# Elementwise sums of y and of W that the planner may give to GpSimd as well as to VectorE

## Chip, core and metric

The kernel runs on one core of a Trainium2 chip. The metric is the device time of one execution in microseconds (us); the median of three runs is quoted. Within the core, TensorE (PE in the profile) multiplies, VectorE (DVE), ScalarE (ACT) and GpSimd (POOL) do elementwise work, and SyncE (SP) issues the DMAs.

## What is computed

The reference, cut to what matters, for two batches of 1024 tokens with 2048 features:

```python
q1 = fake_quant(_layernorm(x), x1_scale, x1_zp)
q2 = fake_quant(ctx_4096, x2_scale, x2_zp)
x = x + jnp.matmul(q1, q2)                      # first product, 2048 x 2048 per batch

n = _layernorm(x)
logits = n @ W_router.T                         # 8 experts, softmax, best 2, weights w
h = jnp.einsum('td,erd->ter', n, lora_A)        # rank 16 per expert
lora = jnp.einsum('ter,eor,te->to', h, lora_B, w) * SCALING
x = x + n @ W_base.T + b_base + lora            # second product, 2048 x 2048
```

## The kernel before

The inputs are fp32; TensorE gets fp16. In the second product each operand is split into a high and a low fp16 part and three products (high x low, low x high, high x high) are accumulated, so each block costs three matmuls. To save matmuls the second product (and the first one of the second batch) uses a Strassen-like scheme: tokens, features and output columns are halved, and seven products of sums and differences take the place of eight. Those sums are what this change is about:

- **Sums of y.** After the second layer norm `y_prep` makes, for each pair p of token tiles, four fp32 tiles of 128 x 1024 (a11, a12, a21, a22) and from them s1, s2, s3 and s4, with four sums by `comb` (L917). `emit` then makes the high part (`affine`, on ACT or DVE), the low part (L910 on DVE), and a DMA transpose.
- **Sums of W.** `w_step(S, b, cp, grp, k)` makes one step's weights: for each of two batches b, two column halves cp, four groups grp and eight k. It loads tiles of W, forms none, one or two sums (L1085 to L1141; 512 or 1024 columns), then the high part `hi` (`affine`, L386 on ACT or L393 on DVE) and the low part `lo` (L1070, a scalar_tensor_tensor on DVE with two SBUF operands).

`g2` then multiplies (L1258) with four token pairs per step; the last k of a group adds the LoRA matmuls (L1274) and evicts PSUM with L1286 on DVE. The accumulators X and Y of four pairs use all eight PSUM banks, so a fresh group waits for the evictions of the one before.

All work is given to a planner, `Plan`, as tasks with estimated durations. A task may be for one engine or for several (`durs` is a dictionary of engine and duration). `rank` gives each task its latest start `prio`, counted back from the matmuls' planned times over durations and hops of 0.7 us (`HOP`). `order` then simulates the engines: at each event it goes over SP, ACT, DVE, POOL and PE in this order, and each free engine takes the ready task with the earliest `prio` that fits into the tile slots. `lag` is how far PE runs behind its planned times. The resulting order is static: each engine executes its own list in order, and semaphores hold it where data is late. Before the change, the only tasks with two engines are for ACT and DVE, and DVE leaves them to ACT when that is free:

```python
if eng == "DVE" and len(t.durs) > 1 and busy["ACT"] <= now:
    continue
```

POOL has only set-up work and the Newton steps of the inverse square root (L432 to L443, then L644 to L646 or L887 to L889), instructions on one or two columns. The work of a batch runs in this order: first product (gemm1), second layer norm and y preparation, router and the first column half of W (cp = 0), second column half (cp = 1), while the next batch is loaded and normalised.

Of the kernel before, what the change touches and what calls it, by code (L numbers as in the profile page):

```python
# [17 lines left out]
ALU = mybir.AluOpType  # L18
# [14 lines left out]
C = 512  # L33
# [49 lines left out]
TURN_LAND = 0.65  # L83
TURN_COST = 0.75
NEXT = {"DVE": 0.08, "ACT": 0.1}


class Buf:
# [18 lines left out]
class Plan:  # L107
# [56 lines left out]
    def order(self):  # L164
# [52 lines left out]
        while todo:  # L217
            if not events:
                raise RuntimeError("no progress")
            nxt = heapq.heappop(events)  # L220
            if nxt <= now:
                continue
            now = nxt
            while releases and releases[0][0] <= now:
                free[heapq.heappop(releases)[-1].tag] += 1
            for eng in busy:
                while busy[eng] <= now:
                    pick = None
                    q = ready[eng]
                    for n, item in enumerate(q):  # L230
                        t = item[2]
                        if t.ready > now:
                            continue
                        h = t.far if t.far is not None else HORIZON
                        if t.prio + lag > now + h:
                            wake(t.prio + lag - h)
                            if t.prio + lag > now + HORIZON:
                                break
                            continue
                        if t.dma is not None:  # L240
                            if dma_free > now + DEPTH:
                                wake(dma_free - DEPTH)
                                break
                            if len([x for x in lanes if x > now]) >= LANES:
                                break
                        if eng == "DVE" and len(t.durs) > 1 and busy["ACT"] <= now:
                            continue
                        if not fits(t):
                            continue
                        pick = t  # L250
                        break
                    if pick is None:
                        break
                    t = pick
                    t.eng, t.dur = eng, t.durs[eng]
                    for e in t.durs:
                        ready[e].remove((t.prio, t.seq, t))
                    for tag, n in t.need.items():
                        free[tag] -= n
                        queue[tag].remove(t)  # L260
                    held.update(t.bufs)
                    t.start = now
                    end = now + t.dur
                    if t.dma is not None:
                        if t.turn:
                            end = max(end, land - 0.2)
                        dma_free = max(end + 0.2, dma_free) + t.dma
                        t.done = dma_free + (
                            TURN_LAND if t.turn else STORE_LAND if t.store else LAND
                        )  # L270
                        land = max(land, t.done)
                        lanes = [x for x in lanes if x > now] + [t.done]
                    else:
                        t.done = end + 0.1
                        end -= NEXT.get(eng, 0.0)
                    busy[eng] = end
                    wake(end)
                    wake(t.done)
                    if t.pe is not None:
                        lag = now - t.pe  # L280
                    for b in t.bufs:
                        b.users -= 1
                        if b.tag in free:
                            b.last = max(getattr(b, "last", 0.0), t.done)
                            if not b.users:
                                heapq.heappush(releases, (b.last, next(count), b))
                                wake(b.last)
                    for s in t.succs:
                        s.left -= 1
                        s.ready = max(s.ready, t.done)  # L290
                        if not s.left:
                            for e in s.durs:
                                bisect.insort(ready[e], (s.prio, s.seq, s))
                            wake(s.ready)
                    todo -= 1
# [4 lines left out]
def xattn_ffn_kernel(ctx, tc, x, cx, scal, wT, bias, arT, bT, out):  # L300
# [78 lines left out]
    def affine(dst, src, n, r, w, scale=None, bias=None, only=None, **kw):  # L379
# [20 lines left out]
        if only:  # L400
            return add(only, durs[only], lambda: fn(only), r=r, w=w, **kw)
        return add(durs, 0, fn, r=r, w=w, **kw)

    def stats(b, s, j, h):
        st = s.ap()[:, j * 24 : (j + 1) * 24].rearrange("p (c s) -> p c s", c=NC)
# [487 lines left out]
    def y_prep(S, b, p):  # L893
# [20 lines left out]
                lambda: n.ap().rearrange("p h c -> p (h c)"), [n], [y], D)  # L914

        def comb(dst, a, c, op):
            add("DVE", 1.22, lambda: nc.vector.tensor_tensor(dst.ap(), a.ap(), c.ap(), op),  # L917
                r=[a, c], w=[dst])

        t1 = norm("a11", 0, 0)  # L920
        emit("a11", t1)
# [135 lines left out]
    def w_step(S, b, cp, grp, k):  # L1057
# [17 lines left out]
        if not cp:  # L1075
            if grp == 0:
                s = kept.pop((cp, k), None) or load_wcol(k, cp, 0, f"wc_{n}", far=WFAR)
            elif grp == 1:
                top = load_wrow(k, cp, f"wt_{n}", far=WFAR)
                s = buf("u", [P, HD], F32, f"wb_{n}", 2)  # L1080
                load(s, lambda: s.ap()[:, :C],
                     wT[(HK + k) * P : (HK + k + 1) * P, cp * HD + C : (cp + 1) * HD],
                     C * 4, [(s, [0])])
                add("DVE", 0.69,
                    lambda: nc.vector.tensor_tensor(  # L1085
                        s.ap()[:, C:], top.ap()[:, C:], top.ap()[:, :C], ALU.subtract),
                    r=[top], w=[(s, [1])])
                add("DVE", 0.69,
                    lambda: nc.vector.tensor_tensor(
                        s.ap()[:, :C], s.ap()[:, :C], s.ap()[:, C:], ALU.subtract), w=[s])  # L1090
            elif grp == 2:
                s = load_wcol(k, cp, 1, f"wc_{n}", far=WFAR)
                add("DVE", 0.69,
                    lambda: nc.vector.tensor_tensor(  # L1094
                        s.ap()[:, :C], s.ap()[:, C:], s.ap()[:, :C], ALU.subtract), w=[s])
            else:
                top = load_wrow(k, cp, f"wt_{n}", far=WFAR)
                s = load_wrow(HK + k, cp, f"wb_{n}", far=WFAR)
                add("DVE", 1.22,
                    lambda: nc.vector.tensor_tensor(s.ap(), s.ap(), top.ap(), ALU.subtract),  # L1100
                    r=[top], w=[s])
                add("DVE", 0.69,
                    lambda: nc.vector.tensor_tensor(
                        s.ap()[:, :C], s.ap()[:, :C], s.ap()[:, C:], ALU.subtract), w=[s])
            hi(lambda: s.ap()[:, :m], 0, m, [s])
            lo(lambda: s.ap()[:, :m], 0, m, [s])
            return
# [5 lines left out]
            return  # L1113
        top = load_wrow(k, cp, f"wt_{n}", far=WFAR)
        if grp == 0:
            add("DVE", 0.69,
                lambda: nc.vector.tensor_tensor(
                    top.ap()[:, C:], top.ap()[:, C:], top.ap()[:, :C], ALU.subtract), w=[top])
            hi(top.ap, 0, HD, [top])
            lo(top.ap, 0, HD, [top])  # L1120
        elif grp == 1:
            bot = buf("u", [P, HD], F32, f"wb_{n}", 2)
            load(bot, lambda: bot.ap()[:, C:],
                 wT[(HK + k) * P : (HK + k + 1) * P, cp * HD + C : (cp + 1) * HD],
                 C * 4, [(bot, [1])])
            add("DVE", 0.69,
                lambda: nc.vector.tensor_tensor(
                    bot.ap()[:, :C], top.ap()[:, :C], top.ap()[:, C:], ALU.subtract),
                r=[top], w=[(bot, [0])])
            add("DVE", 0.69,  # L1130
                lambda: nc.vector.tensor_tensor(  # L1131
                    bot.ap()[:, :C], bot.ap()[:, :C], bot.ap()[:, C:], ALU.add), w=[bot])
            hi(bot.ap, 0, HD, [bot])
            lo(bot.ap, 0, HD, [bot])
        else:
            bot = load_wrow(HK + k, cp, f"wb_{n}", far=WFAR)
            add("DVE", 1.22,
                lambda: nc.vector.tensor_tensor(bot.ap(), bot.ap(), top.ap(), ALU.subtract),
                r=[top], w=[bot])
            add("DVE", 0.69,  # L1140
                lambda: nc.vector.tensor_tensor(  # L1141
                    bot.ap()[:, :C], bot.ap()[:, :C], bot.ap()[:, C:], ALU.subtract), w=[bot])
            hi(bot.ap, 0, HD, [bot])
            lo(bot.ap, 0, HD, [bot])

# [297 lines left out]
```

## Time and profile before

| what | value |
|---|---|
| median of 3 runs | 927.47 us (926.11 to 927.49) |
| profiled execution | 930.89 us, span of its instructions 929.1 us |
| DVE busy | 763.4 us, 82% of the span |
| ACT busy | 418.1 us, 45% |
| POOL busy | 88.8 us, 10% |
| mean granted TensorE clock | 0.992 |

The page gives busy time by engine, and groups of instructions by line, engine and shape with their count, total and mean duration and the idle time of their engine just before them. PEld is the weight load of TensorE. A wait is written "engine line <- what ended it". Idle time of an engine that is not the bottleneck costs nothing by itself.

### The profile page before, as it was taken

The page shows a single profiled execution, that of the slowest core. Times are in us where ns is not written, and L with a number is a line of the kernel's source. Part 1 is how long each engine was busy: PE and PEld are TensorE (multiplying, and loading weights), DVE is VectorE, ACT ScalarE, POOL GpSimd, SP SyncE. Part 2 cuts the span into 40 slices and gives each one's busy share as a digit, 9 for nine tenths or more (in the row PEclk, how much of TensorE's full clock was granted, in tenths as well). Part 3 has the DMA queues.
Part 4 walks back from the last instruction along what each step waited for, and adds up shares of the span by engine and source line. Part 5 has one row for each costly group of instructions (what it writes and reads, how often), then busy time and mean ns, then how long its engine had stood idle before and what let it go on. Part 6 is the DMA issues. An engine that isn't in the chain of part 4 may idle for free.

```text
span 929.1 us, 12550 instructions
## 1 busy us (share of the span) xinstructions
PE 901.3 (97%) x4514; PEld 431.5 (46%) x4514; DVE 763.4 (82%) x1300; ACT 418.1 (45%) x475; POOL 88.8 (10%) x337
## 2 busy tenths in 40 slices
PE   7899998999989999999999999999999999999998
PEld 5444445474434444444444444547443444444443
DVE  7899969999588886999689988899889895699231
ACT  5899558615155331334594665851523221234000
POOL 1425230000000000004440004000000000000000
PEclk8999999999999999999999999999999999999999
DMA  8999999898999998957899926999997879893021
GB/s 321 388 383 265 301 283 249 144 226 279 228 320 320 389 366 289 400 198 246 256 329 277 347 105 178 246 239 221 303 219 244 260 236 382 294 371 119 18 89 48
DMA packets 223183, 241.03 MB, mean 259 GB/s; under 512 B 152464, under 2 KB 154512, under 8 KB 223120
## 3 DMA queue, kind: packets, MB, share of 16 engines
q1 hardware_dynamic: 223120, 240.23, 84.9%
q8 instruction: 35, 0.57, 0.2%
q14 instruction: 28, 0.23, 0.1%
HBM read 172.03 MB, written 31.46 MB: 219 GB/s over the span
## 4 chain that ended last, share of the span: by engine, by line
PE 74%; DVE 10%; DMA 10%; issue 2%; POOL 2%; ACT 1%; SPq 1%; DVEq 0%; POOLq 0%; ACTq 0%
PE X L1258 30%; PE Y L1258 22%; PE g L725 8%; PE gX L845 5%; PE gY L845 3%; DMA wn<-in_wT_dram 2%; PE X L1274 2%; DMA wc<-in_wT_dram 2%; PE ph L958 2%; DVE sm L407 1%; PE Y L1274 1%; DVE yt_a L917 1%; DMA wb<-in_wT_dram 1%; DMA lbs<-in_bT_dram 1%; DMA y_a<-nat_a 1%
## 5 line engine op out<-in xcount | busy, mean ns | idle before, releaser
L1258 PEld LDWEIGHTS <-y_s 128*128 128x128 f16 x1536 | 150.5, 98 | 189.9 <-issue 10.6
L1258 PE MATMUL X<-w,y_s 128*128 128x512 f16 x768 | 208.0, 380 | 6.1 <-DVE w L1070 5.8
L1258 PE MATMUL Y<-w,y_s 128*128 128x512 f16 x768 | 208.0, 381 | 0.2 <-DVE rt L1017 0.2
L1258 PE MATMUL X<-w,y_a 128*128 128x512 f16 x768 | 189.1, 379 | 2.0 <-DMA y_a<-nat_a 0.8
L1258 PEld LDWEIGHTS <-y_a 128*128 128x128 f16 x1152 | 111.9, 98 | 135.5 <-DMA y_a<-nat_a 2.4
L386 ACT ACTIVATE w<-wb,gW 128x1024 f16<-128x1024 f32 (+1 forms) x63 | 64.9, 1038 | 149.1 <-DVE wb L1131 44.0
L725 PE MATMUL g<-b,at 128*128 128x512 f16 x512 | 114.6, 385 | 3.6 <-ACT b L386 3.2
L1258 PE MATMUL Y<-w,y_a 128*128 128x512 f16 x384 | 102.8, 379 | 0.6 <-DMA y_a<-nat_a 0.6
L725 PEld LDWEIGHTS <-at 128*128 128x128 f16 x512 | 50.5, 99 | 64.0 <-issue 4.7
L1070 DVE SCALAR_TENSOR_TENSOR w<-wb,gW,w 128x1024 f16<-128x1024 f32 (+1 forms) x64 | 72.8, 1145 | 7.9 <-ACT w L386 7.8
L1286 DVE SCALAR_TENSOR_TENSOR xr<-X,uW,xr 128x512 f32<-128x512 f32 x64 | 46.6, 744 | 28.4 <-PE X L1274 22.5
L1286 DVE SCALAR_TENSOR_TENSOR xr<-Y,uW,xr 128x512 f32<-128x512 f32 x42 | 31.0, 743 | 37.1 <-PE Y L1274 37.1
L386 ACT ACTIVATE b<-u,nz 128x1024 f16<-128x1024 uint8 x44 | 49.0, 1138 | 8.5 <-DVE bt L816 7.3
L432 POOL TENSOR_SCALAR sm<-sm 128x1 f32<-128x1 f32 (+1 forms) x20 | 4.3, 217 | 468.9 <-DVE sm L419 354.4
L773 ACT ACTIVATE sq<-x,sm 128x1024 uint8<-128x1024 f32 x32 | 36.3, 1136 | 23.6 <-DVE x L754 18.2
L386 ACT ACTIVATE q<-x,sm 128x1024 uint8<-128x1024 f32 x32 | 38.1, 1230 | 15.3 <-POOL sm L646 9.5
L386 ACT ACTIVATE w<-wc,gW 128x1024 f16<-128x1024 f32 x24 | 27.2, 1143 | 39.0 <-DVE wc L1094 28.4
L386 ACT ACTIVATE nat_s<-yt_a 128x1024 f16<-128x1024 f32 x32 | 32.8, 1049 | 25.6 <-DVE yt_a L917 22.7
L407 DVE BATCH_NORM_STATS2 sm<-x 128x6 f32<-128x512 f32 x64 | 40.7, 680 | 2.9 <-DMA x<-in_x_dram 2.9
L386 ACT ACTIVATE u<-bs,sc,rec 128x1024 uint8<-128x1024 f32 x29 | 35.3, 1232 | 13.2 <-DMA bs<-in_cx_dram 12.8
L958 PE MATMUL ph<-ar,y_a 128*128 128x272 f16 x192 | 36.0, 279 | 3.8 <-DMA y_a<-nat_a 3.8
L845 PEld LDWEIGHTS <-at 128*128 128x128 f16 x256 | 25.0, 98 | 30.7 <-issue 0.9
(193 smaller groups left out, 1223.1 us busy)
## 6 DMA issues: line engine op xcount, KB each, us to landing
wt<-in_wT_dram SPq DMA_DIRECT2D x80, 512.0 KB, 7.1
bs<-in_cx_dram SPq DMA_DIRECT2D x64, 512.0 KB, 9.6
wn<-in_wT_dram SPq DMA_DIRECT2D x32, 512.0 KB, 9.2
wb<-in_wT_dram SPq DMA_DIRECT2D x32, 512.0 KB, 7.7
x<-in_x_dram SPq DMA_DIRECT2D x30, 512.0 KB, 7.0
spill<-x SPq DMA_DIRECT2D x28, 512.0 KB, 3.7
xr<-spill SPq DMA_DIRECT2D x28, 512.0 KB, 8.1
wc<-in_wT_dram SPq DMA_DIRECT2D x24, 512.0 KB, 7.9
```

The lines of the kernel that those rows point to most:

```text
L386: nc.scalar.activation(o, i, AF.Copy if c is None else AF.Identity, scale=1.0 if a is None else a, bias=0.0 if c is None else c,)
L407: nc.vector.bn_stats(st[:, 2 * h + c], b.ap()[:, c * C : (c + 1) * C])
L432: e.tensor_scalar(hv, v, -0.5, None, ALU.mult)
L725: nc.tensor.matmul(ps.ap(), aT.ap()[:, k, :], S["b", c, k // 4].ap()[:, k % 4, :], start=k == 0, stop=k == KT - 1,)
L773: nc.scalar.activation(sq.ap(), xb.ap(), AF.Square, bias=a[:, 22 + j : 23 + j], accum_out=a[:, 24 + 2 * j + h : 25 + 2 * j + h],)
L845: nc.tensor.matmul(ps.ap(), a()[:, 4 * h + k, :], w.ap()[:, k, :], start=fresh and h + k == 0, stop=h == 1 and k == 3, skip_group_check=True,)
L917: add("DVE", 1.22, lambda: nc.vector.tensor_tensor(dst.ap(), a.ap(), c.ap(), op), r=[a, c], w=[dst])
L958: nc.tensor.matmul(ph.ap()[:, : 2 * AR], y[half].ap()[:, 0, k, :], ar[:, kr, :], start=kk == 0, stop=False,)
L1070: lambda: nc.vector.scalar_tensor_tensor(w.ap()[:, 1, lo:up], src(), g, w.ap()[:, 0, lo:up], ALU.mult, ALU.subtract),
L1258: nc.tensor.matmul(ps.ap(), y.ap()[:, a, k, :], w.ap()[:, q, j * C : (j + 1) * C], start=k == 0 and fresh and i == 0, stop=k == HK - 1 and ...
L1274: nc.tensor.matmul(ps.ap(), hT.ap()[:, 2 * p + tt, a], lb.ap()[:, q], start=fresh and i == 0, stop=i == 2, skip_group_check=True,)
L1286: nc.vector.scalar_tensor_tensor(xs, ps.ap(), uW[:, cp : cp + 1], xs, ALU.mult, ALU.add)
```

## The change

All elementwise sums of `comb` in `y_prep` and all sums in `w_step` go through a new helper `tt`, which offers the task to DVE and to POOL. POOL's estimate is 3.0 us for 1024 columns (`POOL_T`). In `order`, DVE's rule of leaving a task to ACT now asks whether ACT is among the task's engines, and POOL takes a shared task only if its latest start lies at least 6 us (`SPARE`) ahead; else it looks again when DVE comes free. DVE, which is asked first, takes such a sum whenever it is free and the sum comes first among its ready tasks. The low parts (L910, L1070), the bias sums (L1177) and the sums of `load_lb` stay on DVE alone.

```diff
+SPARE = 6
+POOL_T = 3.0
...
-                        if eng == "DVE" and len(t.durs) > 1 and busy["ACT"] <= now:
+                        if eng == "DVE" and "ACT" in t.durs and busy["ACT"] <= now:
+                            continue
+                        if eng == "POOL" and len(t.durs) > 1 and t.prio + lag < now + SPARE:
+                            wake(busy["DVE"])
                             continue
...
+    def tt(dst, a, c, op, n, r, w, shared=True):
+        def fn(eng):
+            e = nc.gpsimd if eng == "POOL" else nc.vector
+            e.tensor_tensor(dst(), a(), c(), op)
+
+        durs = {"DVE": 0.155 + n * 0.00104}
+        if shared:
+            durs["POOL"] = POOL_T * n / 1024
+            add(durs, 0, fn, r=r, w=w)
+        else:
+            add("DVE", durs["DVE"], lambda: fn("DVE"), r=r, w=w)
...
         def comb(dst, a, c, op):
-            add("DVE", 1.22, lambda: nc.vector.tensor_tensor(dst.ap(), a.ap(), c.ap(), op),
-                r=[a, c], w=[dst])
+            tt(dst.ap, a.ap, c.ap, op, HD, [a, c], [dst])
...
-                add("DVE", 0.69,
-                    lambda: nc.vector.tensor_tensor(
-                        s.ap()[:, :C], s.ap()[:, C:], s.ap()[:, :C], ALU.subtract), w=[s])
+                tt(lambda: s.ap()[:, :C], lambda: s.ap()[:, C:], lambda: s.ap()[:, :C],
+                   ALU.subtract, C, [], [s])
```

The other sums of `w_step` are changed in the same way as the last one.

More of the change, by code (lines that the diff above doesn't have):

```diff
@@ L1083, in w_step @@
                      C * 4, [(s, [0])])
-                add("DVE", 0.69,
-                    lambda: nc.vector.tensor_tensor(
[L1086 to L1090, printed above, removed]
+                tt(lambda: s.ap()[:, C:], lambda: top.ap()[:, C:], lambda: top.ap()[:, :C],
+                   ALU.subtract, C, [top], [(s, [1])])
+                tt(lambda: s.ap()[:, :C], lambda: s.ap()[:, :C], lambda: s.ap()[:, C:],
+                   ALU.subtract, C, [], [s])
             elif grp == 2:
                 s = load_wcol(k, cp, 1, f"wc_{n}", far=WFAR)
-                add("DVE", 0.69,
-                    lambda: nc.vector.tensor_tensor(
-                        s.ap()[:, :C], s.ap()[:, C:], s.ap()[:, :C], ALU.subtract), w=[s])
+                tt(lambda: s.ap()[:, :C], lambda: s.ap()[:, C:], lambda: s.ap()[:, :C],
+                   ALU.subtract, C, [], [s])
             else:
@@ L1098, in w_step @@
                 s = load_wrow(HK + k, cp, f"wb_{n}", far=WFAR)
[L1099 to L1104, printed above, removed]
+                tt(s.ap, s.ap, top.ap, ALU.subtract, HD, [top], [s])
+                tt(lambda: s.ap()[:, :C], lambda: s.ap()[:, :C], lambda: s.ap()[:, C:],
+                   ALU.subtract, C, [], [s])
             hi(lambda: s.ap()[:, :m], 0, m, [s])
@@ L1115, in w_step @@
         if grp == 0:
-            add("DVE", 0.69,
-                lambda: nc.vector.tensor_tensor(
-                    top.ap()[:, C:], top.ap()[:, C:], top.ap()[:, :C], ALU.subtract), w=[top])
+            tt(lambda: top.ap()[:, C:], lambda: top.ap()[:, C:], lambda: top.ap()[:, :C],
+               ALU.subtract, C, [], [top])
             hi(top.ap, 0, HD, [top])
@@ L1125, in w_step @@
                  C * 4, [(bot, [1])])
[L1126 to L1132, printed above, removed]
+            tt(lambda: bot.ap()[:, :C], lambda: top.ap()[:, :C], lambda: top.ap()[:, C:],
+               ALU.subtract, C, [top], [(bot, [0])])
+            tt(lambda: bot.ap()[:, :C], lambda: bot.ap()[:, :C], lambda: bot.ap()[:, C:],
+               ALU.add, C, [], [bot])
             hi(bot.ap, 0, HD, [bot])
@@ L1136, in w_step @@
             bot = load_wrow(HK + k, cp, f"wb_{n}", far=WFAR)
[L1137 to L1142, printed above, removed]
+            tt(bot.ap, bot.ap, top.ap, ALU.subtract, HD, [top], [bot])
+            tt(lambda: bot.ap()[:, :C], lambda: bot.ap()[:, :C], lambda: bot.ap()[:, C:],
+               ALU.subtract, C, [], [bot])
             hi(bot.ap, 0, HD, [bot])
```

## The prediction

> **What bounds the kernel now.** I read the page's busy times first, then the longest waits of TensorE (PE), then busy time by stage, then single durations, then a stretch of the timeline in which VectorE (DVE) and GpSimd (POOL) run side by side.
>
> ```profile
> span 929.1 us, 12550 instructions
> ...
> PE 901.3 (97%) x4514; PEld 431.5 (46%) x4514; DVE 763.4 (82%) x1300; ACT 418.1 (45%) x475; POOL 88.8 (10%) x337
> ```
>
> PE is busy for all but 27.8 us of the span; only that can be won. About 9.4 us of it lie in the first 60 us, where no sum of this change exists, and 4 at the end. That leaves some 14 us. Who ends PE's waits (us in total, times, longest):
>
> ```profile
> PE X L1258 <- DVE w L1070: 6.3, 6, 1.9
> PE ph L958 <- DMA y_a<-nat_a: 3.8, 4, 2.3
> ...
> PE X L1258 <- DMA y_a<-nat_a: 0.8, 1, 0.8
> ...
> PE X L1258 <- DVE x L1286: 0.7, 1, 0.7
> PE Y L1258 <- DMA y_a<-nat_a: 0.6, 1, 0.6
> ```
>
> The first row is a weight step that came late. The y_a rows are y tiles whose transposes came late. Both hang on DVE, so the change aims at the right waits, but these five rows are only 12.2 us. Where DVE is full shows by stage (stretch and length, PE, PEld, DVE, ACT, POOL busy, clock, DMA share, GB/s):
>
> ```profile
> 140.00:250.00 110.00, 107.03 (x650) 58.29 (x648) 100.60 (x153) 54.75 (x60) 0.00 (x0) 1.00 0.98 224
> 250.00:330.00 80.00, 74.89 (x344) 33.44 (x343) 66.34 (x121) 33.61 (x51) 0.00 (x0) 1.00 1.01 337
> 330.00:480.00 150.00, 150.00 (x697) 67.99 (x695) 126.72 (x186) 64.76 (x64) 25.02 (x112) 1.00 0.85 295
> ...
> 580.00:650.00 70.00, 66.95 (x451) 38.99 (x450) 64.99 (x107) 37.73 (x43) 2.77 (x7) 1.00 1.10 238
> 650.00:745.00 95.00, 92.37 (x420) 41.14 (x418) 83.18 (x130) 30.79 (x33) 0.00 (x0) 0.98 0.89 255
> 745.00:860.00 115.00, 115.00 (x535) 52.13 (x533) 96.95 (x115) 34.17 (x36) 0.00 (x0) 1.00 0.77 281
> ```
>
> At 140-330 and 580-745 (y preparation, first weight half, one batch each) PE loses 8.1 and 5.7 us. At 330-480 and 745-860 (second weight half) it loses nothing. The timeline says the same: from the start of a step's split (L1070) to the first matmul with it I read leads of 6.4, 5.6 and 7.6 us around 215-225 us, about 1 us or less around 307-325, 2.5, 0.5 and 3.1 at 656-667, but 20 to 45 us from 356 to 480 and 20 to 55 from 780 on. So a sum of weights is urgent in the first half of a batch's W and idle cargo in the second.
>
> **The change part by part.** The planner's estimate for a sum on DVE is what it was (0.69 and 1.22), so priorities stay. The altered test for ACT leaves the tasks of ACT and DVE as they were. New is that a sum which DVE doesn't take at once goes to POOL if its latest start is at least 6 us (SPARE) off. A 512-wide sum's latest start lies before its matmul by the split (1.28), the half-precision copy (0.75), itself (0.69) and three hops of 0.7: 4.8 us. So POOL takes it only if PE needs the step 10.8 us later or more (12.2 to 12.7 for the first of two sums).
>
> *How many move.* 128 sums of 512 columns and 16 + 16 of 1024 are in w_step (L1085 to L1141), 32 of 1024 in y_prep (L917). By the leads (9 us or more from the split) 85 of the 512-wide and 19 of the 1024-wide W sums are far enough ahead. L917 runs at 163 to 210 and 595 to 652 for matmuls from 210 and 651 on, so most of those are too. As DVE comes first where it is free, I take four in five: 70 of 512, 15 of 1024, and 20 of the 32 L917.
>
> *What DVE gets back.* Durations (busy, mean ns):
>
> ```profile
> L917 DVE TENSOR_TENSOR yt_a<-yt_a,yt_a 128x1024 f32<-128x1024 f32 x32 | 38.5, 1215 | 0.0
> ...
> L1100 DVE TENSOR_TENSOR wb<-wb,wt 128x1024 f32<-128x1024 f32 x16 | 19.5, 1219 | 2.3 <-DMA wb<-in_wT_dram 2.3
> ...
> L1094 DVE TENSOR_TENSOR wc<-wc 128x512 f32<-128x512 f32 x16 | 10.9, 686 | 5.9 <-DMA wc<-in_wT_dram 5.9
> ```
>
> Back to back they start every 1.135 and 0.61 us in the timeline, the ends overlapping. So 70 x 0.61 + 35 x 1.135 = 82 us leave DVE's queue. With them go waits for W's DMAs that stand at its head now (the L1094 row alone has 5.9 us).
>
> *What POOL pays.* No row has a wide two-input sum on POOL. Below: a memset grows from 99 ns (128x2) to 204 (128x128), 0.83 ns a column; two reads at that rate plus the 0.19 of a tiny sum make 1.9 us for 1024. Above: the planner's own 3.0. Between them the Trainium skill (GPSIMD Engine Reference, Performance versus the Vector engine) gives 4497 ns for 2048 columns, from which I estimate 2.25 us for 1024 and 1.15 for 512; no run here shows it yet. POOL gains 70 x 1.15 + 35 x 2.25 = 159 us (134 to 210 by the ends) and goes to about 250 us, 27% of the span. That fits in, if it is free to run. It isn't:
>
> ```profile
> 430.83 0.19 POOL L437 TENSOR_TENSOR sm<-sm 128x1 f32<-128x1 f32 x1
> ...
> 431.03 0.73 DVE L1070 SCALAR_TENSOR_TENSOR w<-ws,gW,w 128x512 f16<-128x512 f32 x1
> 431.11 0.71 POOL L438 TENSOR_TENSOR sm<-sm 128x1 f32<-128x1 f32 x1
> ```
>
> An operation on one column takes 0.19 us alone and 0.71 when DVE has a split with two SBUF operands under way; it ends with the split. Over the trace POOL's one-column sums take 188 to 196 ns beside statistics, PSUM evictions or idle DVE, and up to 1247 beside a 1024-wide split or sum. So DVE shuts POOL out for whole instructions. The reverse can't be seen: POOL's operations are too short. The Trainium skill (SBUF — State Buffer, Who interferes with whom) says that a DVE instruction with two SBUF inputs contends with a GpSimd instruction that reads SBUF, and for such a shared port pair that whoever issues first keeps the other out for the whole instruction. The trace agrees with one direction; the rule speaks against the change, since it makes 159 us of POOL work time in which a split or sum on DVE must wait.
>
> *The two sums.* Without the lock DVE is relieved by 82 us and PE could win part of 12. With it, by stage, POOL time x the share of the stage in which DVE runs two-operand work (from the timeline: 90 of 110 us at 140-250, 79 of 150, 131 of 165 at 580-745, 84 of 115):
> - 140-250: 10 L917 and 8 narrow sums. Relief 16, POOL 32, DVE shut out for 26: 10 us more for a DVE with 9.4 us idle.
> - 580-745: 10 L917, 9 narrow, 2 to 3 wide. Relief 20, POOL 38, shut out 31: 11 us more, against 16.8 idle.
> - 330-480: relief 21, POOL 40, shut out 21: nothing.
> - 745-860: relief 24, POOL 47, shut out 34: 10 more, covered by 18 us idle and leads of 20 us. If this cover went, it would be 10 us of PE.
>
> In the first two stages the 21 us cost PE between 0 (the idle time takes all) and 21 (idle time is waits at the head of the queue and takes none). I take 9, since the leads at 215 and 656 us are only a few us and the idle time lies mostly behind them. Of the 6.3 us of late weight steps I give 1 back: the steps that stall now are the ones with under 10.8 us of lead, and those stay on DVE.
>
> *New waits.* ACT's copy L386 and DVE's split L1070 now wait for POOL. Queued behind L1070 on DVE are the PSUM evictions L1286, for which PE's banks wait; behind a sum waiting for W's DMA on POOL stand the Newton steps of the first layer norm (L432 to L646, 14 chains), for which ACT's q waits. At 330-480 both have leads of 20 us, so I cost them at nothing; without that, each of the 16 group ends could cost 1 to 2 us. Evictions read one SBUF operand and aren't shut out themselves. SP issues the same DMAs; a slot is held about 1 us longer for a moved sum, which I also cost at nothing because the loads run 20 us ahead where most sums move.
>
> Sum: the profiled execution took 930.9 us (span 929.1 and 1.8 around it); +9 - 1 = 938.9. It stood 3.4 above the median of the runs, so on their scale 935.5 us.
>
> **The rivals.**
> - *Faster, 923 us.* The lock lets POOL and DVE alternate at little cost, or POOL's sums fall beside evictions and statistics. DVE then keeps most of 82 us; late steps and late y tiles (6.3 + 5.2) shrink by 4 to 5 us. For it: all waits are DVE's, and DVE no longer stands on W's DMAs. Against: PE's cap of 12, and the 0.71 above. It decides for the change if DVE is shut out for under half of POOL's time.
> - *No difference, 927.5 us.* The sums that move are those of 330-480 and 745-860, where PE has no wait, or the plan puts few on POOL; the change then does less than it says. For it: the 10.8 us rule. Against: L917 has the slack.
> - *Much slower, 950 us.* Back-to-back two-operand work (as at 616-627 us, ten such in a row) starves POOL, sums end several us after their planned 3.0 or 1.5, and the in-order queues pass it on: POOL, ACT's copy, DVE's split, evictions, banks. At 16 group ends x 1.5 us it gives 24 us. It sets in where POOL's sums take more than about twice the plan.
>
> **How the numbers follow.** Moderate loss 0.52 (930 to 945, at 935.5); faster 0.25 (918 to 925.5); no difference 0.12; much slower 0.11 (945 to 965). A measurement can tell about 0.2% here, 1.9 us, so no difference means 925.6 to 929.3. Slower is 0.52 + 0.11 = 0.63. The range from 922 to 953 leaves out the better part of the gains beyond 5.5 us and half of the much slower case. The likeliest case alone is 930 to 945.
>
> **What would show it.** Right: some 100 TENSOR_TENSOR rows on POOL at the old lines' new helper, 512 columns at 1.1 us at best and up to 2.4 with a wait, 1024 at 2.2 and up to 3.5; POOL near 250 us; DVE's busy time near 690, or higher if its records show the shut-out as longer splits; PE's waits for w L1070 or the y tiles grown by about 8 us at 140-330 and 580-745. Wrong: DVE's gaps and durations unchanged beside POOL's sums, PE's waits for w and y_a smaller; or PE losing time in the second halves or at group ends instead.

## The result: 9.5% slower

The changed kernel takes 1015.41 us (median of 4 runs, 1013.32 to 1017.38) against 926.94 us: ratio 1.0955, interval 1.0927 to 1.0983. The direction was the one forecast, the size was not: 88 us lost instead of 8.

The page of the changed kernel, its span and busy times:

```profile
span 1011.5 us, 12627 instructions
...
PE 915.0 (90%) x4514; PEld 436.3 (43%) x4514; DVE 808.4 (80%) x1210; ACT 410.2 (41%) x466; POOL 303.0 (30%) x436
```

99 instructions have left DVE for POOL, and DVE is busier than before, 808.4 us against 763.4. PE now has 96.5 us of idle time (1011.5 - 915.0) where it had 27.8, and its busy time has grown by 13.7 us. Who ends PE's waits after (lines have moved: the evictions are L1288, the split L1086, the sums L412):

```profile
PE ph L974 <- DVE xr L1288: 25.3, 2, 15.0
PE Y L1260 <- DVE xr L1288: 19.1, 4, 9.7
PE X L1260 <- DVE w L1086: 17.5, 8, 5.2
PE X L1260 <- DVE w L398: 5.5, 1, 5.5
PE X L1260 <- ACT w L391: 3.7, 2, 1.9
PE X L1260 <- DVE x L1288: 3.6, 1, 3.6
```

The two largest rows did not exist before: PE waits for PSUM evictions, in single waits of up to 15 us. Late weight steps (17.5 against 6.3) come third. Why DVE is late shows in its groups and POOL's (busy, mean ns):

```profile
L412 POOL TENSOR_TENSOR yt_a<-yt_a,yt_a 128x1024 f32<-128x1024 f32 x25 | 71.5, 2871 | 54.2 <-ACT yt_a L391 22.8 <-DVE nat_a L927 16.4 <-DVE yt_a L412 8.4
L412 POOL TENSOR_TENSOR wb<-wb 128x512 f32<-128x512 f32 x32 | 57.0, 1782 | 135.3 <-DVE wb L412 105.3 <-DMA wb<-in_wT_dram 27.8 <-ACT w L391 1.2
...
L1086 DVE SCALAR_TENSOR_TENSOR w<-wb,gW,w 128x1024 f16<-128x1024 f32 x48 | 78.4, 1644 | 10.6 <-ACT w L391 9.0 <-DMA wt<-in_wT_dram 1.2
L1288 DVE SCALAR_TENSOR_TENSOR xr<-X,uW,xr 128x512 f32<-128x512 f32 x64 | 46.5, 742 | 23.8 <-PE X L1276 23.1 <-PE X L1260 0.7
L927 DVE TENSOR_TENSOR nat_a<-yt_a,nat_a 128x1024 f16<-128x1024 f32 x24 | 41.8, 1757 | 0.1
```

The same groups of DVE before the change:

```profile
L1070 DVE SCALAR_TENSOR_TENSOR w<-wb,gW,w 128x1024 f16<-128x1024 f32 x48 | 60.9, 1278 | 6.2 <-ACT w L386 6.1
L1286 DVE SCALAR_TENSOR_TENSOR xr<-X,uW,xr 128x512 f32<-128x512 f32 x64 | 46.6, 744 | 28.4 <-PE X L1274 22.5 <-PE X L1258 5.8
...
L910 DVE TENSOR_TENSOR nat_a<-yt_a,nat_a 128x1024 f16<-128x1024 f32 x24 | 28.8, 1218 | 0.0
```

DVE's instructions with two SBUF operands have become longer (split 1644 ns against 1278, low part 1757 against 1218). The eviction, with one SBUF operand and one in PSUM, is as short as before (742 against 744). Side by side in the timeline of the y preparation:

```profile
188.72 9.79 POOL L412 TENSOR_TENSOR yt_a<-yt_a,yt_a 128x1024 f32<-128x1024 f32 x3 [2.36 <-DVE yt_a L412]
189.64 3.38 DVE L927 TENSOR_TENSOR nat_a<-yt_a,nat_a 128x1024 f16<-128x1024 f32 x1
192.94 3.36 DVE L927 TENSOR_TENSOR nat_s<-yt_a,nat_s 128x1024 f16<-128x1024 f32 x1
196.23 3.38 DVE L927 TENSOR_TENSOR nat_a<-yt_a,nat_a 128x1024 f16<-128x1024 f32 x1
```

Three POOL sums in 9.79 us and three low parts of 1.22 us that now take 3.38: the engines take turns, one whole instruction each. In about 10 us the two engines together do six of them, which DVE alone does in 6.8 us. And the place where PE pays, at the end of that y preparation:

```profile
208.48 0.74 DVE L1288 SCALAR_TENSOR_TENSOR xr<-X,uW,xr 128x512 f32<-128x512 f32 x1
...
210.40 0.73 DVE L1288 SCALAR_TENSOR_TENSOR xr<-Y,uW,xr 128x512 f32<-128x512 f32 x1
...
211.19 0.39 PE L974 MATMUL ph<-ar,y_a 128*128 128x272 f16 x1 [10.31 <-DVE xr L1288]
```

The first eviction runs here at 208.5 us. Before, it ran at 186.7, and DVE had stood idle for it:

```profile
186.74 0.75 DVE L1286 SCALAR_TENSOR_TENSOR xr<-X,uW,xr 128x512 f32<-128x512 f32 x1 [0.96 <-PE X L1258]
```

PE needs the bank that these evictions free. It executes its list in order, so nothing behind this matmul can start.

### The profile page after: what moved, and what is told of

Same layout as the page of the kernel before. It is cut to its first block, busy times and chain, and to the rows that moved or that the text cites. A ratio compares the mean times of both kernels' runs of the same rounds, so it can differ in the third digit from the quotient of the medians.

```text
span 1011.5 us, 12627 instructions
## 1 busy us (share of the span) xinstructions
PE 915.0 (90%) x4514; PEld 436.3 (43%) x4514; DVE 808.4 (80%) x1210; ACT 410.2 (41%) x466; POOL 303.0 (30%) x436
## 4 chain that ended last, share of the span: by engine, by line
PE 47%; DVE 32%; DMA 10%; issue 7%; POOL 3%; ACT 1%; SPq 1%; DVEq 0%; POOLq 0%; ACTq 0%
PE X L1260 16%; PE Y L1260 10%; DVE w L1086 7%; PE g L742 7%; PE gX L862 5%; PE gY L862 4%; DVE wb L412 3%; DVE nat_s L927 3%; DVE xr L1288 3%; DMA wb<-in_wT_dram 3%; PE ph L974 2%; DVE nat_a L927 2%; DVE xr L1179 2%; DMA wt<-in_wT_dram 2%; PE X L1276 1%
## 5 line engine op out<-in xcount | busy, mean ns | idle before, releaser
L391 ACT ACTIVATE w<-wb,gW 128x1024 f16<-128x1024 f32 (+1 forms) x58 | 59.9, 1035 | 162.4 <-DVE wb L412 92.0
L1260 PE MATMUL Y<-w,y_a 128*128 128x512 f16 x384 | 107.8, 394 | 19.1 <-DVE xr L1288 19.1
L1086 DVE SCALAR_TENSOR_TENSOR w<-wb,gW,w 128x1024 f16<-128x1024 f32 (+1 forms) x64 | 94.1, 1481 | 13.2 <-ACT w L391 11.6
L412 POOL TENSOR_TENSOR wb<-wb 128x512 f32<-128x512 f32 x32 | 57.0, 1782 | 135.3 <-DVE wb L412 105.3
L412 POOL TENSOR_TENSOR yt_a<-yt_a,yt_a 128x1024 f32<-128x1024 f32 x25 | 71.5, 2871 | 54.2 <-ACT yt_a L391 22.8
L742 PEld LDWEIGHTS <-at 128*128 128x128 f16 x512 | 50.6, 99 | 63.6 <-issue 4.6
L1288 DVE SCALAR_TENSOR_TENSOR xr<-X,uW,xr 128x512 f32<-128x512 f32 x64 | 46.5, 742 | 23.8 <-PE X L1276 23.1
L974 PE MATMUL ph<-ar,y_a 128*128 128x272 f16 x192 | 39.5, 296 | 27.6 <-DVE xr L1288 25.3
L1288 DVE SCALAR_TENSOR_TENSOR xr<-Y,uW,xr 128x512 f32<-128x512 f32 x42 | 31.0, 740 | 41.0 <-PE Y L1276 41.0
L927 DVE TENSOR_TENSOR nat_s<-yt_a,nat_s 128x1024 f16<-128x1024 f32 x32 | 48.7, 1549 | 0.0
L1179 DVE TENSOR_TENSOR xr<-xr,bb 128x1024 f32<-128x1024 f32 x28 | 41.1, 1484 | 6.4 <-DMA bb<-in_bias_dram 6.4
L412 POOL TENSOR_TENSOR wb<-wb,wt 128x1024 f32<-128x1024 f32 x13 | 37.1, 2856 | 30.2 <-DMA wb<-in_wT_dram 29.2
```

The lines of the kernel that those rows point to most:

```text
L391: nc.scalar.activation(o, i, AF.Copy if c is None else AF.Identity, scale=1.0 if a is None else a, bias=0.0 if c is None else c,)
L412: e.tensor_tensor(dst(), a(), c(), op)
L742: nc.tensor.matmul(ps.ap(), aT.ap()[:, k, :], S["b", c, k // 4].ap()[:, k % 4, :], start=k == 0, stop=k == KT - 1,)
L927: lambda: nc.vector.tensor_tensor(n.ap()[:, 1], t.ap(), n.ap()[:, 0], ALU.subtract), r=[t], w=[n])
L974: nc.tensor.matmul(ph.ap()[:, : 2 * AR], y[half].ap()[:, 0, k, :], ar[:, kr, :], start=kk == 0, stop=False,)
L1086: lambda: nc.vector.scalar_tensor_tensor(w.ap()[:, 1, lo:up], src(), g, w.ap()[:, 0, lo:up], ALU.mult, ALU.subtract),
```

## The experiments

Three theories. *Port*: POOL's sums shut DVE out, DVE's list falls behind the plan, and the evictions in it have no lead. *Order*: the new order itself is bad, whatever runs it. *Late sums*: POOL ends its sums late, and ScalarE and DVE wait for them. The kernel before had a median of 929.03 us beside the first four kernels below (all sums on VectorE, write only, y alone, W alone) and 929.52 beside the others.

### The changed order with all sums on VectorE

```diff
-            e = nc.gpsimd if eng == "POOL" else nc.vector
-            e.tensor_tensor(dst(), a(), c(), op)
+            nc.vector.tensor_tensor(dst(), a(), c(), op)
```

> The changed kernel's order is kept, but the 99 sums that its plan gives to GpSimd are issued by VectorE at the same place of the plan. Three theories. Port: GpSimd's wide sums shut VectorE's two-operand work out (133 us of longer instructions: busy time 808.4 against 763.4, though 88 us of sums had left), VectorE's list falls behind the plan, and the PSUM evictions in that list have no lead. Here the 133 us go and about 80 us of sums come back, so the lag shrinks to 80/133: some 50 us over the kernel before, 975 us (960 to 985). Order: the new order itself, with more work ahead of the evictions, costs the time whatever engine runs it: near 1015 us. Late sums: ScalarE and VectorE wait for sums that end late on GpSimd: these waits are gone, 927 to 940 us.

967.12 us, ratio 1.0388 (1.0340 to 1.0436), 38 us lost. The long waits are still there, shorter (PE's waits of this kernel):

```profile
PE ph L973 <- DVE xr L1287: 19.5, 2, 10.3
PE X L1259 <- DVE w L1085: 7.3, 8, 2.0
PE Y L1259 <- DVE xr L1287: 6.5, 4, 4.6
```

Durations are as before the change (the split 1282 ns), and no sum is on POOL. So late sums are not what is left here. In all, DVE does hardly more than before (769.3 us busy against 763.4). But the order was made for a DVE with some 80 us less to do, and with the whole work in it, it costs 38 us: what the relief was to bring, the planner had already spent by putting other work ahead of the evictions.

### GpSimd only writes

```diff
-            e = nc.gpsimd if eng == "POOL" else nc.vector
-            e.tensor_tensor(dst(), a(), c(), op)
+            if eng != "POOL":
+                nc.vector.tensor_tensor(dst(), a(), c(), op)
+                return
+            nc.gpsimd.memset(dst(), 0.5)
+            nc.gpsimd.memset(dst(), 0.25)
+            nc.gpsimd.memset(dst()[:, : n // 2], 0.5)
```

> The changed kernel's plan and all its waits, but each of the 99 sums on GpSimd is replaced by two and a half memsets of the same tile, so GpSimd writes the tile for as long (an estimated 2.4 us for 1024 columns, 1.35 for 512, from the memset rows) and reads nothing; these sums are left out of the computation. Port (by the read side): VectorE's splits and low parts go back to 1279 and 1217 ns, its busy time to about 675 us, PE loses less than before the change: 915 to 930 us. Order, or late sums: near 1015 us. If the write side locks as well, VectorE's instructions stay stretched and the time stays over 990 us.

929.43 us, ratio 0.9998 (0.9983 to 1.0012): all of the loss is gone, with the same plan and POOL busy for 267.6 us. From its page, and its groups on POOL and DVE:

```profile
PE 899.1 (97%) x4514; PEld 430.8 (46%) x4514; DVE 695.1 (75%) x1210; ACT 409.6 (44%) x466; POOL 267.6 (29%) x634
```
```profile
L415 POOL MEMSET yt_a<- 128x1024 f32 x25 | 25.1, 1004 | 1.4
...
L1090 DVE SCALAR_TENSOR_TENSOR w<-wb,gW,w 128x1024 f16<-128x1024 f32 x48 | 60.9, 1280 | 13.3 <-ACT w L391 13.1
...
L931 DVE TENSOR_TENSOR nat_a<-yt_a,nat_a 128x1024 f16<-128x1024 f32 x24 | 28.8, 1218 | 0.2 <-ACT nat_a L391 0.2
```

The split is back at 1280 ns and the low part at 1218, so it is POOL's reading that shuts DVE out. Order as a cause by itself falls: it is the same here and costs nothing once DVE is relieved and not shut out.

Late sums do not fall by this run. A memset waits only for the tile that it writes, so POOL's waits before the sums of y shrink from 54.2 us to 19.0, and it ends earlier. They are judged by who waits in the changed kernel; DVE's waits there, and below them the row of ScalarE's copies before the change:

```profile
DVE w L1086 <- ACT w L391: 16.1, 18, 2.3
...
DVE nat_s L396 <- POOL wb L412: 1.2, 1, 1.2
```
```profile
DVE w L1070 <- ACT w L386: 12.5, 15, 1.3
```

DVE waits for a sum of POOL for 1.2 us, and for ScalarE's copies hardly longer than before; here, without a loss, it waits for them for 23.4 us. PE waits for such copies for 3.7 us in the changed kernel. By these waits, late sums are worth a few us of the 88 at most.

With one plan in both, the difference of DVE's busy times is the shut-out: 808.4 - 695.1 = 113 us. (The 133 of the expectations compared it with another plan; this plan also gives some high parts from ScalarE to DVE.)

The second finding is that nothing is won either. DVE has 68 us less to do than before, and PE's idle time stays (27.5 us, 27.8 before). Late weight steps shrink from 6.3 to 3.6 us, others grow (qn of the start, the sum of squares, hT). DVE stands at W's DMAs instead (its waits):

```profile
DVE wb L412 <- DMA wt<-in_wT_dram: 30.4, 15, 6.7
...
DVE wb L412 <- DMA wb<-in_wT_dram: 14.3, 13, 2.9
```

Before the change the corresponding rows had 9.9 and 3.1 us for wt, 8.2, 2.3 and 1.6 for wb. The measured time is at the upper end of the 915 to 930 us that were expected.

### One part alone: sums of y, sums of W

```diff
-    def tt(dst, a, c, op, n, r, w, shared=True):
+    def tt(dst, a, c, op, n, r, w, shared=False):
...
-            tt(dst.ap, a.ap, c.ap, op, HD, [a, c], [dst])
+            tt(dst.ap, a.ap, c.ap, op, HD, [a, c], [dst], shared=True)
```

> Only the sums of y may go to GpSimd (25 of 32 do); the sums of W are on VectorE alone. The evictions of the changed kernel fall behind by 22 us at 187-209 us and by 23 at the same place of the second batch, so Port expects 45 us over the kernel before, 972 us (955 to 985), with the long waits of PE on L1288 at these two places and none in the second weight halves. Order or late sums: no rule by part; for late sums some 10 us, since few wait for s1 to s4.

971.73 us, ratio 1.0443 (1.0392 to 1.0494), 43 us. The other half has `shared=True` for W and `shared=False` in `comb`:

> Only the sums of W may go to GpSimd (15 of 1024 and 59 of 512 columns do); the sums of y are on VectorE alone. Port expects the other part: 82 - 45 = 37 us over the kernel before, 964 us (950 to 980), with PE's waits for evictions at the ends of the second weight halves' groups (11 us each) and a few us at each weight step stage. Late sums: this is the part for which ScalarE waited 68 us, so nearly all of the loss, over 990 us.

966.67 us, ratio 1.0375 (1.0317 to 1.0433), 38 us. PE's waits, y alone and then W alone:

```profile
PE ph L974 <- DVE xr L1288: 24.2, 2, 13.8
PE X L1260 <- DVE w L1086: 11.2, 6, 5.1
```
```profile
PE Y L1260 <- DVE xr L1288: 18.5, 3, 11.7
PE X L1260 <- DVE w L1086: 7.7, 6, 1.9
```

The two add up to 80 of the 88 us, and each has the waits of its own stage. How late single evictions are, in us after the same eviction before the change (read from the timelines; the head gives the time before). Lateness adds up, so a stage costs the step from one column to the next:

| kernel | 186.7 | 369.9 | 410.7 | 630.2 | 806.6 | 851.9 | 924.4 |
|---|---|---|---|---|---|---|---|
| changed | 21.8 | 33.7 | 46.1 | 67.7 | 72.6 | 84.6 | 82.3 |
| its order on DVE | 11.0 | 19.5 | 25.6 | 35.1 | 33.1 | 38.1 | 35.8 |
| POOL writes only | -0.2 | 0.7 | 2.4 | -1.5 | -2.4 | -1.9 | -2.4 |
| y alone | 21.2 | 19.0 | 19.4 | 41.8 | 39.8 | 39.8 | 39.8 |
| W alone | 0.6 | 3.5 | 19.4 | 15.4 | 26.6 | 38.0 | 35.6 |

The 25 sums of y cost 21 and 22 us in the two batches' y preparations. The sums of W cost 16 us between 370 and 411 and 11 between 807 and 852, in the second weight halves, where W was 20 to 55 us ahead, and another 11 between 630 and 807, mostly in the second batch's first weight half.

### Only sums of W with 20 us of slack

```diff
-SPARE = 6
+SPARE = 20
...
-            tt(dst.ap, a.ap, c.ap, op, HD, [a, c], [dst])
+            tt(dst.ap, a.ap, c.ap, op, HD, [a, c], [dst], shared=False)
```

> Only sums of W, and only with 20 us of slack in the plan instead of 6: 10 of 1024 and 31 of 512 columns go to GpSimd. If slack of the sum protects, as the prediction had it for the second weight halves, nothing is lost: 925 to 930 us. If the loss lies in VectorE's list behind the shut-out instruction, slack of the sum is no help: some 60 to 70 us of sums on GpSimd cost as they do where all sums of W may go (36 us for 143 us there), so 16 to 18 us over the kernel before: 945 us (938 to 953).

953.79 us, ratio 1.0264 (1.0231 to 1.0297): 24 us for 41 sums, more than the 16 to 18 expected and nothing like no loss. PE's first wait:

```profile
PE Y L1260 <- DVE xr L1288: 19.4, 2, 12.3
```

Slack of the sum is no protection: the sum can wait, but the DVE instruction that it shuts out cannot.

### The planner knows of the shut-out

```diff
                     busy[eng] = end
+                    if eng == "POOL" and len(t.durs) > 1:
+                        busy["DVE"] = max(busy["DVE"], now) + 0.65 * t.dur
+                        wake(busy["DVE"])
```

With all sums shared:

> As the changed kernel, but the planner charges VectorE 0.65 of each sum's planned duration when GpSimd takes it (133 us of stretch over 205 us planned). The plan then gives GpSimd more sums: 54 of 1024 and 79 of 512 columns, 227 us by the shortest records against 166. If the loss is a plan that doesn't know of the shut-out, the evictions now stand where VectorE can reach them in time: 930 to 950 us in spite of the longer shut-out. If VectorE simply has too much to do (over 180 us of shut-out against some 115 us of relief), no order helps: over 1000 us.

978.93 us, ratio 1.0540 (1.0513 to 1.0567). Neither case: more sums are on POOL (busy 367.1 us), yet the loss is 49 us instead of 88. Evictions have left the head of PE's waits (the one row left has 0.5 us); late weight steps have taken their place:

```profile
PE X L1263 <- DVE w L1089: 15.3, 10, 5.7
PE X L1263 <- ACT w L394: 13.2, 4, 6.5
```

So with the charge PE hardly waits for evictions. Why the weight steps are late is not settled. It is not DVE's load by itself: DVE is busy for 756.9 us, less than the 763.4 before. The two longest waits for ScalarE's copies (6.5 and 4.7 us) follow two stands of DVE before the bias sums (11.2 and 5.9 us), with the sum that this step needs queued behind them (at the second, W's own DMA was late too); before the change this row had 4.1 us:

```profile
DVE xr L1182 <- DMA bb<-in_bias_dram: 17.2, 2, 11.2
```

With fewer sums the charge can be seen more clearly: the same with W alone and 20 us of slack:

> Only sums of W with 20 us of slack, as in the run that lost 24 us, but the planner charges VectorE 0.65 of a sum's planned duration when GpSimd takes it. The plan then moves 16 sums of 1024 and 42 of 512 columns instead of 10 and 31. If the loss is that evictions stand behind work that the plan believed done, it all but goes although the shut-out grows by a third or more: 927 to 937 us, and PE's long waits for L1288 are gone. If it is VectorE's total work, more sums cost more: 955 to 970 us.

937.29 us, ratio 1.0072 (1.0046 to 1.0098). With 58 sums on POOL instead of 41 the loss falls from 24 to 8 us, just above the 927 to 937 us that were expected, and no eviction is among PE's waits. The first two rows:

```profile
PE X L1263 <- DVE w L1089: 5.6, 3, 2.3
PE ph L977 <- DMA y_a<-nat_a: 3.3, 2, 2.7
```

### One read instead of two

```diff
-            e = nc.gpsimd if eng == "POOL" else nc.vector
-            e.tensor_tensor(dst(), a(), c(), op)
+            if eng == "POOL":
+                nc.gpsimd.tensor_copy(dst(), a())
+            else:
+                nc.vector.tensor_tensor(dst(), a(), c(), op)
```

> The changed kernel's plan, with each of the 99 sums on GpSimd replaced by a copy of its first operand (the sums are left out of the computation): one read and one write instead of two reads and one write. If any read by GpSimd shuts two-operand work on VectorE out, its stretch falls only with the duration: an estimated 1.0 to 1.3 us for 1024 columns, about half, so 940 to 975 us. If it takes two reads, as the write-only run: 926 to 932 us.

945.79 us, ratio 1.0168 (1.0137 to 1.0199), 16 us lost. One line of its page:

```profile
PE 905.7 (96%) x4514; PEld 432.7 (46%) x4514; DVE 729.0 (77%) x1210; ACT 410.4 (43%) x466; POOL 212.6 (23%) x436
```

DVE is busy for 34 us more than where POOL only writes, and single splits are up to 0.77 us longer. One read is enough.

No version beat the kernel before, and none is in sight on this path: the run in which POOL shuts nobody out is no faster either.

## Why the prediction was right in direction and wrong in size

- *Which waits, how many sums.* 70 narrow, 15 wide and 20 of y were expected to move; 61, 13 and 25 did. By the pitches of 0.61 and 1.135 us that relieves DVE of 80 us, against 82.
- *POOL's price.* The estimates of 2.25 and 1.15 us were near: the shortest records are 2.34 and 1.26. With waits the means are 2.87 and 1.75, so POOL came to 303 us instead of 250.
- *The lock.* The row of 0.19 and 0.71 us had shown one direction (the 1247 ns beside it is an operation on two columns; the longest on one took 1052). The other direction of the rule that it cites held for two-operand work, for whole instructions. The stage sums gave 26 + 31 + 21 + 34 = 112 us of shut-out, and 113 was measured, but that they met is in part luck. In the trace before, two-operand work without a PSUM operand fills 83, 122, 74 and 79 us of the same four stages instead of 90, 131, 79 and 84, which makes the sum 104. And by stage the shut-out was about 36 (up to 330 us), 42, 16 and 22 us, by DVE's durations in the changed kernel less those where POOL only writes, between the same evictions.
- *The step that failed* is the next one, from DVE's shut-out to PE: a net 21 us in the tight stages, 9 of them on PE, 1 us of late weight steps given back, and nothing in the second halves. It went wrong in two places. First, relief was set against shut-out. The planner knows of the relief and fills it with work ahead of the evictions; it doesn't know of the shut-out. So in the tight stages the shut-out stood almost gross against DVE's idle time. Up to the first eviction (the kernel before, its order on DVE, POOL writes only, changed; stretch, length, then busy time and count of PE, PEld, DVE, ACT and POOL, clock, DMA, GB/s):

```profile
0.00:186.74 186.74, 174.23 (x919) 87.97 (x920) 160.87 (x375) 137.02 (x160) 43.81 (x161) 0.97 0.99 291
```
```profile
0.00:197.67 197.67, 178.97 (x939) 90.57 (x940) 174.30 (x387) 137.90 (x161) 43.15 (x161) 0.96 0.97 283
```
```profile
0.00:186.50 186.50, 172.89 (x919) 87.26 (x920) 160.78 (x374) 137.64 (x161) 75.85 (x200) 0.97 0.99 294
```
```profile
0.00:208.48 208.48, 180.96 (x939) 90.68 (x940) 184.01 (x374) 138.16 (x161) 78.09 (x174) 0.93 0.93 273
```

  13 sums have left DVE by then, some 15 us, yet its work ahead of the eviction is as long as before (160.8 against 160.9 us): in its order on DVE, 9 more sums of y and 3 more low parts stand there. The shut-out of 23 us comes on top whole, and the eviction is 22 us late. That knowing of the shut-out helps is shown by the planner's charge (a loss of 8 us instead of 24).

  Second, "covered by leads of 20 us" took the lead of weight steps for that of DVE. Evictions stand in the same list, have no such lead, and fell back by another 12 us in each second half (33.7 to 46.1 and 72.6 to 84.6 in the table). The prediction had named them as queued behind L1070 and then cost them at nothing. Measured by PE's waits, evictions cost 47 us more than before, and late weight steps (w L1086, w L398 and ScalarE's copies) 20 us more instead of 1 less.
- *A missing term.* The rest is PE's busy time: it grew by 13.7 of the 82.4 us by which the span grew. In the stretches with the two longest waits the clock fell (columns: stretch, length, PE, PEld, DVE, ACT, POOL, clock, DMA, GB/s):

```profile
200.00:225.00 25.00, 14.69 (x117) 10.88 (x115) 15.58 (x18) 2.00 (x4) 4.20 (x2) 0.73 1.01 239
675.00:700.00 25.00, 10.04 (x49) 4.84 (x48) 25.00 (x18) 4.85 (x5) 12.32 (x5) 0.76 1.08 219
```

  That the waits lowered the clock is read from their coincidence; no run parts the two.
- *The rivals.* Faster, by up to 12 us: even without the lock the gain was nil. No difference: too few sums would have had to move. Much slower at 950 us was nearer, but by another way: it put the loss on POOL's late sums, for which DVE waited 1.2 us. Its last links, DVE's splits and the evictions behind them, were right.

What stays open: how much of the 88 us a plan that knows of the shut-out would save with these 99 sums. The charge to the planner halved the loss, but it changed the set too, and the weight steps that were late then are explained only in part.

## What to carry to other kernels

Before giving work to another engine, ask what its instruction stops, not only whether the instruction itself has slack: here sums with 20 us to spare delayed evictions that had none. In a static order, delay that the plan doesn't know is paid by the instruction with the least lead in that engine's list, and relief that the plan does know can be spent on other work (up to the first eviction all of it was). And before relieving an engine, take the work away for a run: here that gave 929.4 us against 929.0, so there was nothing to win.

## What the runs showed of the hardware that was not expected

That sums on GpSimd and two-operand instructions on VectorE take strict turns, one whole instruction each (1.22 us became 3.38), was forecast. These were not in the prediction's sums:

- GpSimd's writes alone left VectorE's durations as they were (1280 and 1218 ns).
- VectorE's fp32 to fp16 copies, with one SBUF operand, were held as well when they met a sum of GpSimd (L396 up to 2629 ns, 688 on average before; L398 up to 2847, 753 before).
- VectorE's smallest instructions paid as much as the wide ones. Here are one-column steps beside POOL's sums of y; the first and the last were held, the one between was not. Instructions on one or two columns make up some 17 of the 113 us, and these stand ahead of the weight step (w L398) for which PE then waits 5.5 us:

```profile
148.92 1.65 DVE L452 SCALAR_TENSOR_TENSOR sm<-sm 128x1 f32<-128x1 f32 x1
...
151.24 0.22 DVE L452 SCALAR_TENSOR_TENSOR sm<-sm 128x1 f32<-128x1 f32 x1
...
151.50 2.23 DVE L457 SCALAR_TENSOR_TENSOR sm<-sm 128x1 f32<-128x1 f32 x1
```

- The 13 evictions that ran wholly inside a sum of GpSimd took 732 to 746 ns, as ever.
